# Turning twelve 128x512 tiles by blocks on VectorE and a trip through memory, or on TensorE

## The chip, the cores and the metric

The kernel runs on one core of one Trainium2 chip. The metric is the time of one execution in device microseconds. Three runs of the kernel before took 1243.22, 1246.52 and 1256.35 us; the median is 1246.52 us.

## The reference

Two layers work on eight sequences (B = 8) of 128 tokens of 512 values. The first is a per-sequence linear map, followed by a base linear layer with a gated mixture of eight low-rank experts. The second, in which the change lies, is attention over a paged cache followed by a gated low-rank layer:

```python
q, k = rope(rmsnorm(x @ Wq.T)), rope(rmsnorm(x @ Wk.T))   # 32 query heads, 8 key heads of 128
scores = q @ concat(k_cache[pages], k).T * SCALE           # 512 cached keys and 128 new ones
o = softmax(where(valid, scores, -1e30)) @ concat(v_cache[pages], v)
y = o.reshape(b, s, 4096) @ Wo.T                           # the attention's output, 128 x 512 per sequence
gate = softmax over the top 16 of (y @ Wq_w.T) @ keys.T    # 64 experts
z_gated = (y @ A_w.T).reshape(64, 8) * gate
x = x + (z_gated @ B_w.T) * SCALING
```

For each sequence the second layer's last part needs two tiles with their axes exchanged: y (the attention's output) ahead of the products with the router and A_w, and z_gated ahead of the product with B_w. TensorE contracts over the partitions, so a 128x512 tile with tokens on the partitions has to be turned into four 128x128 pieces with features on the partitions.

## The kernel before, in words

All engines follow an order written out by hand: each engine executes its instructions in the order in which the program records them.

The attention is cut into 64 units (NU). A unit is one sequence and one key head; there are four passes (NQ) over the eight sequences, with two key heads (GH) in each pass. A step `st` is one sequence of one pass, `st = u // 2`. The function `iteration(u)` (called for u = 0 to 66) overlaps the stages of several units:

- The scores of unit u on TensorE, for four query heads (`scores`, L793 and L796), each into one of two PSUM buffers of two banks. VectorE adds the mask and takes the minimum (`mask_exp`, L806), which frees the buffer; ScalarE takes the exponential (L817); GpSimd divides by the sum (`normalize`, L823).
- VectorE then turns the probabilities by blocks of 32x32 (`blocks`, L828), and `exchange_out` writes them to DRAM in four DMAs, two issued by SP and two by ScalarE (tile `px`, L840). In the next iteration `exchange_in` loads them back on SP with the blocks at their exchanged places (`pT`, L853). The turned queries and keys of unit u + 2 travel in the same way and are loaded first (`qkb`, L850); ScalarE copies them into order in `heads_qk` (L860) in iteration u + 1, ready for the scores of iteration u + 2.
- `values` (L873) multiplies the turned probabilities of unit u - 2 with the cached values, at the end of an iteration. ScalarE copies the result out of PSUM (`evict_o`, L884), and `output` (L895) multiplies it with Wo. After a step's second head `add_output` (L916) adds the new partial sum to that of the earlier passes; earlier passes keep theirs in DRAM (`yd`, `load_y`, L143). In the last pass the finished y of sequence b appears in iteration 52 + 2b.
- The projections for later units (`project`, L259 and L262), their norms (`norms`: squares on ScalarE L308, then `rs` on GpSimd L312 and L314) and the rotation on VectorE (`rotate`, L326 to L344; `rotate_k`, L340, needs `rs`) fill the rest.
- SP loads the cached key pages with one small DMA each (`gather`, L194), after it has read the page's number (L193).

The last layer begins while the attention still runs. `LAST` places sequence b = 0 to 6 in iteration 59 + b: `f_turn` turns y with four transposes on TensorE into PSUM (L684), which ScalarE copies to `yT` (L686); `f_project` makes the router's scores (L692) and z (L701); `f_gate` on VectorE, with one exponential on ScalarE (L724), makes `zg` (L733). In iterations 59 to 63 `f_turn` stands at the third head, later at the beginning. `z_turn` turns `zg` by four more transposes (L746) and a copy (L748), in iteration 65 and 66 for sequences 0 and 1 and in the tail for the others. The tail's `f_second` multiplies with B_w (L1130), adds the first layer's x (L1137) and writes the result (L1140).

The tile `y_home`, free from iteration 50 on, holds the finished y of sequences 0 to 3 and later the turned z of 0 and 1. The tile `xo` holds the projections' left operands; the last projection reads it in iteration 58. The tile `rooms` holds `zg` and the small tiles of the gate.

A DMA that SP or ScalarE issues signals one of eight completion semaphores. The program assigns them in turn over both queues, and a DMA waits for the one that used its semaphore before, unless that is known to be done.

Of the kernel before, what the change touches and what calls it, by code (L numbers as in the profile page):

```python
# [9 lines left out]
F32 = mybir.dt.float32  # L10
I32 = mybir.dt.int32
AF = mybir.ActivationFunctionType
ALU = mybir.AluOpType
# [3 lines left out]
P = 128  # L17
B = 8
S = 128
DM = 512  # L20
NC = DM // P
# [9 lines left out]
GH = 2  # L31
NQ = HKV // GH
HW = NH // 2 * D + D
QD = P // 32
# [23 lines left out]
def adaln_ffn_kernel(  # L58
# [25 lines left out]
    nc = tc.nc  # L84
# [49 lines left out]
    xo = keep.tile([P, B // 2, 7, 2, S], F32, name="xo")  # L134
# [4 lines left out]
    ya_t = {}  # L139
# [43 lines left out]
    def gather(step, first=0, end=NPP):  # L183
        hf, b = divmod(step, B)
        if first == 0:
            kv_t[step] = (
                kvp.tile([P, NPP, GH, PSIZE], F32, tag="kt", name=f"kt_{step}"),
                kvp.tile([P, LC, GH * D], F32, tag="vt", name=f"vt_{step}", bufs=3),
            )
        kt, vt = kv_t[step]  # L190
        for j in range(first, end):
            at = b * NPP + j
            page = nc.sync.value_load(pg[0:1, at : at + 1])  # L193
            nc.sync.dma_start(  # L194
                out=kt[:, j, :, :].rearrange("p g t -> p (g t)"),
                in_=kc[hf, ds(page, 1)].rearrange("o p f -> p (o f)"),
            )
# [17 lines left out]
    def bank(tag, name):  # L215
        return ps_1.tile([P, DM], F32, tag=tag, name=name)
# [454 lines left out]
    def f_fold(psum):  # L671
# [5 lines left out]
            )  # L677
        nc.vector.tensor_copy(fw_t["s"], rk)

    def f_turn(b, sb, psum):  # L680
        yb = ya_t.pop((NQ - 1) * B + b)
        tp = psum("tp", [P, NC, S])
        for c in range(NC):
            nc.tensor.transpose(tp[:, c, :], yb[:, c * P : (c + 1) * P], ident)  # L684
        yT = sb("yT", [P, NC, S])
        nc.scalar.copy(yT, tp)  # L686
        return yT
# [52 lines left out]

    zT_t = {}

    def z_turn(b, tp, sb):
        zg = zg_t.pop(b)
        for c in range(NC):
            nc.tensor.transpose(tp[:, c * S : (c + 1) * S], zg[:, c * P : (c + 1) * P], ident)  # L746
        zT = sb("zT", [P, NC, S])
        nc.scalar.copy(zT.rearrange("p c s -> p (c s)"), tp)  # L748
        zT_t[b] = zT


    with ExitStack() as l1:
# [150 lines left out]
        def add_output(u):  # L903
            st, g = units[u]
            del oT_t[u]
            if g % GH < GH - 1:
                return
            y = y_t.pop(st)
            last = st >= (NQ - 1) * B
            if g < GH:  # L910
                ya_t[st] = yp.tile([P, DM], F32, tag="ya", name=f"ya_{st}")
                nc.vector.tensor_copy(ya_t[st], y)
            else:

                t = y_home[st % B] if last and st % B < 4 else ya_t[st]
                nc.vector.tensor_tensor(t, y, ya_t[st], ALU.add)  # L916
                ya_t[st] = t
            if not last:
                nc.sync.dma_start(out=y_d[st % B], in_=ya_t.pop(st))

# [1 line left out]

        LAST = {NU - 5 + b: b for b in range(B - 1)}
        y_home, yT_t, room_t = {}, {}, {}

        def rooms():
            w = wp.tile([P, 7 * 2 * HW], F32, tag="wqkv", name="rooms", bufs=GH)
# [31 lines left out]
        def iteration(u):  # L959

            on = lambda v: 0 <= v < NU
            fb = LAST.get(u)
            r, group = u % 16, (u // 16 + 1) * GH
            f = room(fb) if fb is not None else None

            if u % 4 == 3:
                k, j, four = (u + 5) // 4, 0, True
            elif u % 4 == 0:
                k, j, four = (u + 4) // 4, 0, False
            elif u % 4 == 1:  # L970
                k, j, four = (u + 3) // 4, 1, True
            else:
                k, j, four = (u + 2) // 4, 1, False
            slots = ()
            if 2 < u and k < NU // 4:
                slots = (1, 2, 6) if four else (4, 5, 3)
            st = u // GH
            pages = on(u) and 1 < st + 1 < NQ * B
            first, end = ((0, 10), (10, NPP))[u % GH]
            if pages:  # L980
                gather(st + 1, first, first + 3)
            if on(u - 1):
                exchange_in(u - 1)
            if pages:
                gather(st + 1, first + 3, end)
            if pages:
                gather_v(st + 1, u % GH * LC // GH, (u % GH + 1) * LC // GH)
            if on(u + 3) and u % GH == 1:
                make_tables(units[u + 3][0])
            if u % GH == 0 and B <= st - 1 < NQ * B:  # L990
                load_y(st - 1)
            if on(u - 3):
                evict_o(u - 3)
            if u >= NU and fb is not None:
                yT_t[fb] = f_turn(fb, *f)
            if u > NU:
                z = u - NU - 1
                z_turn(z, bank("q" if z else "kv", f"ztp_{z}"), lambda n, shape: y_home[
                    z
                ].rearrange("p (c s) -> p c s", c=NC))  # L1000
            for h in range(REP):
                if on(u):
                    scores(u, h)
                    mask_exp(u, h)
                    if h > 0:
                        normalize(u, h - 1)

                    if h == 1:
                        if u == 2:
                            rotate(4)  # L1010
                        elif u == 3:
                            sums_q(1, 3, 2)
                        elif u == 4:
                            sums_q(1, 4, 1)
                        elif r in (10, 11, 12, 13) and u < NU - 8:
                            sums_q(group + r // 12, *((3, 2), (4, 1))[r % 2])
                    if h == 2:
                        new_pb(u)
                        if u + 2 in range(3, NU):
                            blocks_qk(u + 2, u)  # L1020
                    if h > 1:
                        blocks(u, h - 2)
                    if h == 1 and u == NU - 5:
                        f_fold(f[1])
                    if h == 2 and fb is not None:
                        yT_t[fb] = f_turn(fb, *f)
                if on(u - 3):
                    output(u - 3, h)
                if h > 0 and slots:
                    project(k, j, slots[h - 1 : h])  # L1030

                if u < 3 and h in (1, 3):
                    project_whole(1, *[(0, 1, h // 2), (1, h // 2, 1), (1, h // 2, 0)][u])
            if on(u - 3):
                add_output(u - 3)
            if on(u + 1) and (u + 1) % GH == 0:
                make_mask(units[u + 1][0])
            if u + 1 in range(3, NU):
                heads_qk(u + 1)

            if u < NU - 8:
                if r in (8, 9, 10, 11):
                    load_q(group + r // 10, r % 2, r % 2 + 2)
                if r in (12, 13):
                    load_o(group, r % 2 * 2, r % 2 * 2 + 2)
            if 16 < u < NU and r in (1, 2):
                load_o(group - 1, r * 2 - 2, r * 2)
            if NU - 8 < u < NU - 2:
                f_weights(u - NU + 7)
            if u == 2:  # L1050
                sums_q(0, 1)
            if on(u):
                normalize(u, REP - 1)
            if u == 0:
                norms(4)
            elif 4 < u + 3 < NU:
                norms(u + 3)
            if on(u):
                blocks(u, REP - 2)
                blocks(u, REP - 1)  # L1060
                exchange_out(u)
            if 4 < u + 3 < NU:
                rotate(u + 3)
                if four and slots:
                    project(k, j, (7,))

            if u in (2, 5, 7, 9):
                sums_x({2: 2, 5: 3, 7: 0, 9: 1}[u])
            if u == NU - 14:
                t = wp.tile([P, 4 * DM], F32, tag="wo", name="y_home", bufs=GH + 1)  # L1070
                y_home.update({b: t[:, b * DM : (b + 1) * DM] for b in range(4)})
            if u == NU - 6:
                rooms()
            if fb is not None:
                f_gate(fb, *f_project(fb, yT_t.pop(fb), *f), *f)
            if on(u - 2):
                values(u - 2)

# [6 lines left out]
    with ExitStack() as l2:  # L1085
# [31 lines left out]
        def f_turn_z(t):  # L1117
            b = t
            sb = lambda n, shape: p2.tile(shape, F32, tag=n, name=f"f{n}_{b}")
            z_turn(b, bank("q" if t % 2 else "kv", f"ztp_{t}"), sb)  # L1120

        def f_second(t):
            b = t
# [114 lines left out]
```

## Time and profile before

| | before |
|---|---|
| median of three runs | 1246.52 us |
| the profiled execution | 1243.45 us |
| its span, first to last instruction | 1241.7 us |
| TensorE busy | 1224.1 us, 99% |
| VectorE busy | 902.4 us, 73% |
| ScalarE busy | 506.6 us, 41% |
| GpSimd busy | 590.7 us, 48% |
| granted TensorE clock | 0.997 |
| DMA | 298.99 MB, 241 GB/s on average |
| exchange out `px`, issue to landing | 5.5 us (SP), 6.4 us (ScalarE) |
| exchange in `pT`, `qkb` | 6.6 us, 3.4 us |

The profile gives the busy time of each engine as a share of the span. Matmuls are pipelined: a row's own duration is longer than the time by which it moves the next one, so what a matmul costs is read from the chain of waits. That chain is followed back from the last instruction, at each step to what released it; time off this chain costs nothing until it grows enough to get on it. The profile's iterations near the end begin at 1087.7 us (59), 1105.8 (60), 1122.6 (61), 1139.4 (62), 1156.2 (63), 1173.1 (64), 1186.1 (65) and 1199.2 (66 has its y matmuls from here, and the tail follows).

### The profile page before, as it was taken

The numbers are of one execution on the slowest core, as the hardware profiler recorded it, in microseconds if no ns is written. First come the engines' busy times: TensorE is split into PE (matmuls) and PEld (weight loads), VectorE is DVE, ScalarE is ACT, GpSimd is POOL, SyncE is SP. The second block draws the span as 40 slices with busy tenths as digits, with TensorE's granted clock in tenths as the row PEclk, the third lists the DMA queues.
The fourth block names the chain that finished last, engine by engine and source line by source line (L and its number), as shares of the span: only waits on it lengthen the run. The fifth ranks groups of instructions, "written<-read, shape, count | busy, mean of one in ns | idle before, by whom it ended". The sixth has DMA issues, their size and how long they took to land.

```text
span 1241.7 us, 15991 instructions
## 1 busy us (share of the span) xinstructions
PE 1224.1 (99%) x3847; PEld 650.6 (52%) x3847; DVE 902.4 (73%) x2045; ACT 506.6 (41%) x1457; POOL 590.7 (48%) x687
## 2 busy tenths in 40 slices
PE   8999899999999999999999999999999999999998
PEld 7765455554555555555455555554555555555444
DVE  2546798889877777788877777788777777787522
ACT  1334444444444444444444444444444444443211
POOL 2443565575544555555445545655445544553100
PEclk9999999999999999999999999999999999999999
DMA  8822777788878877888878778888878777787512
GB/s 303 304 79 94 223 233 249 234 274 286 271 234 257 259 244 249 284 277 281 266 258 268 252 243 260 287 284 275 257 242 281 248 235 231 259 269 269 178 51 85
DMA packets 204785, 298.99 MB, mean 241 GB/s; under 512 B 84563, under 2 KB 116564, under 8 KB 203796
## 3 DMA queue, kind: packets, MB, share of 16 engines
q1 hardware_dynamic: 173092, 205.41, 52.6%
q10 hardware_dynamic: 18720, 52.49, 12.0%
q0 software_dynamic: 12880, 40.08, 9.4%
q8 instruction: 31, 0.51, 0.2%
q14 instruction: 62, 0.51, 0.1%
HBM read 183.54 MB, written 114.36 MB: 240 GB/s over the span
## 4 chain that ended last, share of the span: by engine, by line
PE 88%; DVE 4%; DMA 3%; ACT 2%; issue 1%; POOL 1%; ACTq 1%; SPq 0%; DVEq 0%; POOLq 0%
PE o L873 19%; PE p L259 18%; PE y L895 16%; PE s L793 16%; PE s L796 4%; PE p L292 2%; PE bp L517 2%; PE op L1130 2%; PE cp L495 2%; PE fz L701 2%; DMA px<-pb 1%; DVE wqkv L163 1%; ACT sq L308 1%; DMA kt<-in_kc 1%; DVE p L806 1%
## 5 line engine op out<-in xcount | busy, mean ns | idle before, releaser
L823 POOL TENSOR_SCALAR p<-p,den 128x640 f32<-128x640 f32 x256 | 211.8, 827 | 424.0 <-DVE den L822 423.4
L817 ACT ACTIVATE p<-p,low 128x640 f32<-128x640 f32 x256 | 212.0, 828 | 437.3 <-DVE den L822 297.4
L806 DVE CUSTOM_DVE_ANT_0 p<-s,mask,rs 128x640 f32<-128x640 f32 x256 | 224.0, 879 | 109.1 <-PE s L796 106.0
L259 PE MATMUL p<-wqkv,xo 128*128 128x384 f32 x784 | 280.4, 486 | 0.0
L895 PE MATMUL y<-wo,oT 128*128 128x512 f32 x512 | 262.5, 597 | 5.4 <-ACT oT L884 5.4
L793 PE MATMUL s<-kt,qkT 128*128 128x512 f32 x504 | 258.6, 595 | 3.2 <-ACT qkT L860 2.7
L873 PE MATMUL o<-pT,vt 128*128 128x512 f32 x512 | 230.2, 592 | 0.0
L259 PEld LDWEIGHTS p<-wqkv,xo 128*128 128x128 f32 x784 | 148.9, 190 | 139.8 <-issue 73.1
L828 DVE STREAM_TRANSPOSE pb<-p 128x640 f32<-128x640 f32 x252 | 207.7, 824 | 16.9 <-POOL p L823 16.9
L796 PEld LDWEIGHTS s<-qkT 128*128 128x128 f32 x504 | 96.2, 191 | 121.1 <-issue 121.1
L873 PEld LDWEIGHTS o<-pT,vt 128*128 128x128 f32 x512 | 97.3, 190 | 110.3 <-issue 95.2
L204 POOL DMA_INDIRECT vt<-in_vc,vrow x128 | 135.9, 1062 | 39.3 <-issue 27.7
L793 PEld LDWEIGHTS s<-kt,qkT 128*128 128x128 f32 x504 | 95.5, 191 | 98.2 <-issue 55.0
L314 POOL TENSOR_TENSOR rs<-ss,mhalf 128x5 f32<-128x5 f32 x64 | 99.7, 1558 | 5.3
L308 ACT ACTIVATE sq<-c 128x128 f32<-128x128 f32 x320 | 98.8, 309 | 8.1
L796 PE MATMUL s<-qkT 128*128 128x128 f32 x504 | 97.2, 275 | 0.0
L884 ACT COPY oT<-o 128x512 f32<-128x512 f32 x64 | 37.5, 586 | 144.8 <-PE o L873 139.4
L895 PEld LDWEIGHTS y<-wo,oT 128*128 128x128 f32 x512 | 78.6, 192 | 11.4 <-ACT oT L884 6.8
L262 DVE TENSOR_TENSOR c<-c,p 128x384 f32<-128x384 f32 x84 | 45.3, 539 | 31.2 <-PE p L259 31.2
L873 PE MATMUL o<-pT,vn 128*128 128x512 f32 x128 | 65.4, 592 | 0.0
L308 ACT ACTIVATION_READ_ACCUMULATOR sq<-c 128x1 f32 x320 | 59.7, 186 | 0.0
L779 DVE STREAM_TRANSPOSE pb<-ca 128x640 f32<-128x640 f32 x61 | 50.5, 828 | 6.8 <-DMA px<-pb 5.9
(181 smaller groups left out, 1178.9 us busy)
## 6 DMA issues: line engine op xcount, KB each, us to landing
pT<-px SPq DMA_DIRECT2D x64, 1280.0 KB, 6.6
px<-pb SPq DMA_DIRECT2D x122, 400.0 KB, 5.5
px<-pb ACTq DMA_DIRECT2D x122, 400.0 KB, 6.4
qkb<-px SPq DMA_DIRECT2D x61, 320.0 KB, 3.4
kt<-in_kc SPq DMA_DIRECT2D x512, 32.0 KB, 4.6
wqkv<-in_wqkv POOLq DMA_DIRECT2D x32, 384.0 KB, 5.1
yd<-ya SPq DMA_DIRECT2D x24, 256.0 KB, 3.1
wo<-in_wo POOLq DMA_DIRECT2D x12, 512.0 KB, 4.5
```

Source lines behind the costliest of these rows:

```text
L204: nc.gpsimd.indirect_dma_start(out=kv_t[step][1][:, c, :], out_offset=None, in_=vc, in_offset=bass.IndirectOffsetOnAxis(ap=vrow[:, hf, at ...
L259: nc.tensor.matmul(out=ps, lhsT=xo[:, pr, x, c, :], rhs=w[:, c, :], start=(c == 0), stop=(c == 1))
L308: nc.scalar.activation(sq, cs[:, at : at + D], AF.Square, accum_out=ss[:, h : h + 1])
L314: nc.gpsimd.tensor_tensor(rs, ss, mhalf, ALU.pow)
L793: nc.tensor.matmul(out=s[:, :L], lhsT=qkT[:, h, :], rhs=kt[:, :, g % GH, :], start=True, stop=True)
L796: nc.tensor.matmul(out=s[:, L:NK], lhsT=qkT[:, h, :], rhs=qkT[:, REP, :], start=True, stop=True)
L806: nc.vector.tensor_tensor_reduce(out=p, in0=s_t.pop((u, h))[:, :NK], in1=mask_t[st], scale=rs_t[u][:, h : h + 1], scalar=BIG, op0=ALU.add, ...
L817: nc.scalar.activation(p, p, AF.Exp, bias=low, scale=-1.0, accum_out=den)
L823: nc.gpsimd.tensor_scalar(p_t[u, h], p_t[u, h], den, 1.0, ALU.mult, ALU.mult)
L828: nc.vector.transpose(pb_t[u][:, :, h * w : (h + 1) * w].rearrange("p i (j a) -> p j i a", a=32), p_t.pop((u, h)).rearrange("p (j i a) -> ...
L873: nc.tensor.matmul(out=o, lhsT=vt[:, c, j * D : (j + 1) * D] if c < LC else vn_t.pop(u), rhs=pT[:, c], start=(c == 0), stop=(c == LC),)
L895: nc.tensor.matmul(out=y_t[st], lhsT=oT_t[u][:, h, :], rhs=wo_t[g][:, h, :], start=(h == 0 and j == 0), stop=(h == REP - 1 and j == GH - 1),)
```

## The change

For sequences 0 to 5 (`TURNED`) both y and zg are turned in another way. VectorE exchanges each 32x32 block's axes in one instruction (`turn_blocks`), four DMAs on SP write the result to DRAM with rows of 512 bytes, one DMA on SP loads it back with the blocks at their exchanged places (`turn_in`), and ScalarE copies it into the order of the matmuls (`turn_chunks`). Sequences 6 and 7 still go through TensorE.

The turn of y follows directly on the unit's `exchange_out` in iteration 52 + 2b, that of zg on the gate in iteration 59 + b. The load back stands in the next iteration after SP's page loads. The turned blocks of y 0 to 3 lie in `y_home`, those of y 4 and 5 and of all zg in `xo`; the sum L916 now stays in its own tile.

```diff
+    def turn_blocks(n, rows, room, pool):
+        nc.vector.transpose(
+            room.rearrange("p (k c a) -> p c k a", k=QD, c=NC),
+            rows.rearrange("p (c k a) -> p c k a", c=NC, k=QD),
+        )
+        m = pool.tile([QD, 32, QD, NC * 32], F32, tag="yx", name=f"yx_{n}")
+        for i in range(QD):
+            nc.sync.dma_start(
+                out=m[:, :, i].rearrange("k b f -> b k f"),
+                in_=room[i * 32 : (i + 1) * 32].rearrange("p (k f) -> p k f", k=QD),
+            )
+        blocks_t[n] = m, room
+
+    def turn_in(n):
+        m, room = blocks_t.pop(n)
+        nc.sync.dma_start(
+            out=room.rearrange("p (i f) -> p i f", i=QD), in_=m.rearrange("k b i f -> (k b) i f")
+        )
+        turned_t[n] = room
+
+    def turn_chunks(n, out):
+        nc.scalar.copy(
+            out.rearrange("p c (i a) -> p c i a", a=32),
+            turned_t.pop(n).rearrange("p (i c a) -> p c i a", i=QD, c=NC),
+        )
...
     def f_turn(b, sb, psum):
+        if ("y", b) in turned_t:
+            yT = sb("yT", [P, NC, S])
+            turn_chunks(("y", b), yT)
+            return yT
...
-    def z_turn(b, tp, sb):
+    def z_turn(b, sb):
         zg = zg_t.pop(b)
+        if ("z", b) in turned_t:
+            zT = zT_t[b] = sb("zT", [P, NC, S])
+            turn_chunks(("z", b), zT)
+            return
+        tp = bank("q" if b % 2 else "kv", f"ztp_{b}")
...
-                t = y_home[st % B] if last and st % B < 4 else ya_t[st]
-                nc.vector.tensor_tensor(t, y, ya_t[st], ALU.add)
-                ya_t[st] = t
+                nc.vector.tensor_tensor(ya_t[st], y, ya_t[st], ALU.add)
...
             if pages:
                 gather(st + 1, first + 3, end)
+            for n in list(blocks_t):
+                turn_in(n)
...
                 exchange_out(u)
+            b = (u - 3) // GH - (NQ - 1) * B
+            if on(u - 3) and (u - 3) % GH and 0 <= b < TURNED:
+                place = y_home[b] if b < 4 else spare[:, (b + 2) * DM : (b + 3) * DM]
+                turn_blocks(("y", b), ya_t.pop((NQ - 1) * B + b), place, dram_x)
...
                 f_gate(fb, *f_project(fb, yT_t.pop(fb), *f), *f)
+                if fb < TURNED:
+                    turn_blocks(("z", fb), zg_t[fb], spare[:, fb * DM : (fb + 1) * DM], dram_x)
```

More of the change, by code (lines that the diff above doesn't have):

```diff
@@ L678, in f_fold @@
         nc.vector.tensor_copy(fw_t["s"], rk)
+    blocks_t, turned_t = {}, {}
+    TURNED = B - 2
+    def turn_blocks(n, rows, room, pool):
[21 more added lines that the diff above has]
+        )
     def f_turn(b, sb, psum):
+        if ("y", b) in turned_t:
+            yT = sb("yT", [P, NC, S])
+            turn_chunks(("y", b), yT)
+            return yT
         yb = ya_t.pop((NQ - 1) * B + b)
@@ L924, in adaln_ffn_kernel @@
         y_home, yT_t, room_t = {}, {}, {}
+        spare = xo.rearrange("p r x c s -> p (r x c s)")
         def rooms():
@@ L997, in iteration @@
                 z = u - NU - 1
-                z_turn(z, bank("q" if z else "kv", f"ztp_{z}"), lambda n, shape: y_home[
-                    z
-                ].rearrange("p (c s) -> p c s", c=NC))
+                z_turn(z, lambda n, shape: y_home[z].rearrange("p (c s) -> p c s", c=NC))
             for h in range(REP):
@@ L1119, in f_turn_z @@
             sb = lambda n, shape: p2.tile(shape, F32, tag=n, name=f"f{n}_{b}")
-            z_turn(b, bank("q" if t % 2 else "kv", f"ztp_{t}"), sb)
+            z_turn(b, sb)
         def f_second(t):
```

## The prediction

> **What bounds the kernel now.** I read the busy shares first, then the chain of waits over the last 150 us, then the timelines of VectorE, ScalarE and the SP queue where the change works. The page:
>
> ```profile
> PE 1224.1 (99%) x3847; PEld 650.6 (52%) x3847; DVE 902.4 (73%) x2045; ACT 506.6 (41%) x1457; POOL 590.7 (48%) x687
> ...
> PE 88%; DVE 4%; DMA 3%; ACT 2%; issue 1%; POOL 1%; ACTq 1%; SPq 0%; DVEq 0%; POOLq 0%
> ```
>
> TensorE is the bound and is almost never idle. The granted clock is 0.997 throughout, so only removed matmul time or new stalls count. The chain (start, length, what) shows the pieces to be removed:
>
> ```profile
> 1093.92 0.44 PE ftp L684 x4
> ...
> 1173.13 0.59 ACT oT L884
> 1173.72 0.04 issue
> 1173.76 3.70 PE y L895 x8
> ...
> 1186.08 0.44 PE ftp L684 x4
> 1186.52 0.44 PE ztp L746 x4
> 1186.95 3.56 PE y L895 x8
> ...
> 1199.22 0.59 ACT oT L884
> ```
>
> A sequence's four transposes cost 0.44 us of chain. Two groups are not in it: turning y 5 (near 1173) and z 1 (near 1199) stands beside the ScalarE copy L884, for which the next y matmul waits anyway. Iteration u of the loop starts at its first scores: 59 at 1087.7, 60 at 1105.8, 61 at 1122.6, 62 at 1139.4, 63 at 1156.2, 64 at 1173.1.
>
> Three timelines (start, length) around iterations 59 and 60 show the slack: VectorE,
>
> ```profile
> 1107.65 0.69 DVE L733 TENSOR_TENSOR rooms<-fz,rooms 128x512 f32<-128x512 f32 x1
> 1108.26 0.88 DVE L806 CUSTOM_DVE_ANT_0 p<-s,mask,rs 128x640 f32<-128x640 f32 x1
> ```
>
> ScalarE,
>
> ```profile
> 1098.34 0.71 ACT L860 COPY qkT<-qkb 128x640 f32<-128x640 f32 x1
> ```
>
> and SP's queue:
>
> ```profile
> 1094.44 0.53 SPq L850 DMA_DIRECT2D qkb<-px  x1
> ...
> 1108.50 0.54 SPq L850 DMA_DIRECT2D qkb<-px  x1
> ```
>
> VectorE goes from the gate straight into the first mask step (L806) of iteration 60, which ends at 1109.14; its PSUM bank is what the third head's scores need, and they start at 1109.49. That is 0.35 us of slack. In iteration 61 it is 1126.05 against 1126.31. The qkb load needs 3.4 us to land, so the one of 1094.44 lands 0.5 us before ScalarE copies it.
>
> **What is removed.** By the order of the instructions 48 TensorE transposes go (12 groups), 12 VectorE transposes and 60 DMAs on SP (48 out, 12 back) come. The gains by the chain:
> - y 0 to 4, in iterations 59 to 63: 5 x 0.44 = 2.2 us.
> - y 5 and z 1: nothing, as above.
> - z 0 at 1186.52: the y matmuls would start at 1186.78 (end of the L884 copy, 1186.17 + 0.59 + 0.02) instead of 1186.95: 0.2 us.
> - z 2 to 5, between output matmuls with no gap: 4 x 0.44 = 1.76 us. ScalarE's copies from memory come earlier than those from PSUM, none is late.
> Together 4.1 us, with 5.2 us (12 x 0.44) as the upper bound. The 128x128 transpose has rows of 272 ns each, but four take 0.44 us, so 0.11 us of the chain each. The Trainium skill ("TensorE: Matmul & The Clock Gate", Part 4: PE-mode transpose) gives about 275 ns in a kernel's context; that is the row, but 48 x 0.275 = 13.2 us would be three times what the chain gives back. The Trainium skill ("VectorE: DVE Perf Modes", Rules for kernel authors) would leave a 128x128 transpose on TensorE where PSUM may receive it, against this change; no row of before weighs the two, as only what TensorE waits for decides here.
>
> **What is added on VectorE and ScalarE.** A 128x640 block transpose steps by 0.74 us (L828), so 128x512 takes 0.59. The six of y follow the last blocks of an even iteration; there rotate_k waits 0.5 us (iterations 52 to 58) or 1.4 us (60) for POOL's rs, and the later mask step has over 2 us to its bank, so nothing reaches TensorE. The z ones stand between the gate and the mask step: 0.35 us of slack in 60 and 0.26 in 61 are overrun, in 62 and 63 VectorE idles 2.6 and 3.0 us before that step. ScalarE's copies of 128x512 keep their number; the permuted one takes 0.57 (L860: 0.71 for 640) where the PSUM one takes 0.57.
>
> **What is added on SP's queue.** Every hardware DMA signals one of eight semaphores in turn, and waits for the DMA that used it before. In the order of the changed program this does three things:
> 1. After each y turn (even iterations), four out-DMAs stand ahead of the next iteration's three page loads and its qkb load, and those page loads now wait for the exchange px, eight places back. An issue costs 0.4 us (rows 0.33 to 0.42). Before, the page loads were issued while px was on its way; now they come after it, 0.68 us each. Iteration 53: qkb 994.29 becomes about 996, lands 999.4, and was copied at 999.45: hidden. In 55 and 57 alike (slack 1.7). In 59 the px landing (7.4 us from 1086.51) lets the first load go at 1093.9, three make it 1095.6 instead of 1094.44: 1.15 us late, 0.65 over the slack. The copy, the norms, rs, rotate_k, the gate and the mask step of 60 all follow it.
> 2. The four z out-DMAs of iteration 59 wait on SP for the VectorE turn, which is after the gate: 1108.3 + 0.65 + 0.66 = 1109.6, issued by 1111.2. Behind them are three page loads (2.0 us as after an exchange; 5.1 us, the stretch 987.7 to 992.8, while one is in flight; I take 2.8, nearer to the first since px has landed) and qkb, so 1114.0 instead of 1108.50, landing 1117.4 where it was copied at 1115.16: 2.3 us late, with 1.4 to 4.5 as ends.
> 3. The load back of z 0 in 60 waits for ScalarE's first px DMA of 60, and SP's own two px DMAs are queued behind it. Px goes out in two steps, its halves one landing (4.6 us) apart, then the z 1 out-DMAs, page loads and qkb for 62: about 1137 to 1140, where it was 1125.41 + 3.4. The copy ran at 1131.98, but its reader, the scores of 62, came at 1139.4. This uses nearly all of that cover; I cost it at nothing.
>
> **The sum.** Iteration 60, third head: the bank is free at 1109.14 + 0.59 + 0.65 + 0.25 (from mask end to scores, the waiting weight load included) = 1110.6; TensorE would be there at 1109.49 - 0.44 = 1109.05; stall 1.6. Iteration 61: free at 1126.05 + 0.25 + 0.59 + 2.3 = 1129.2; TensorE would be there at 1126.31 - 0.88 + 1.6 = 1127.0; stall 2.2 (1.3 to 4.4). Lost 3.8, gained 4.1: net -0.3 us. The profiled execution took 1243.45 us (its span 1241.7), so 1243 us. It is 3 us under the median of the three runs, 1246.52, whose spread (1243.22 to 1256.35) is larger than the change; I stay with 1243 and let the range reach up.
>
> **The rivals.**
> - *A clean gain.* The page loads go out fast and POOL's rs, not qkb, still sets the gate; only the turns' 0.59 us overrun. By the sum's formula without the 0.65 and the 2.3 they make stalls of 0.9 and 0.5 us; with the ready bank used a little sooner, none. 1243.45 - 4.1 + 0 to 1.5 = 1239.3 to 1240.9. For it: landings vary from 4.1 to 7.4 us, and SP waits for px 98 us in 76 waits, so it has time. Against it: only 1.2 to 1.4 us of wait remain at the qkb loads of 53 to 59.
> - *The exchange falls behind: slower.* One mechanism: the px of 60 in two steps. If a landing takes 7.4 us (the row of 1086.5) and three page loads 5.1, then ScalarE's px of 60 lands at 1127.5, SP's at 1136.5, qkb goes at 1142 and is copied by 1146.3; the scores of 62 are due at 1139.4 + 2.5 = 1141.9, so 4.4 us are lost. The point is a landing of qkb after 1141.2; from there each us is a us of TensorE. SP's second px of 61 then waits for ScalarE's px of 61, which stands behind that copy: the scores of 63 lose some 3 us more. With the stalls of 60 and 61 at their upper end (6.5): -4.1 + 6.5 + 7.4 = +9.8, 1253 us; +12.4 is needed for 1%, so two landings must be longer yet.
> - *The change does nothing*: excluded by the order of the instructions, which lacks the 48 transposes.
>
> **How the numbers follow.** A measurement of this kernel tells 1% (12 us) from no change. Forecast (1241 to 1246): 0.5. Clean gain (1238 to 1241, 5.2 us being the bound): 0.25. Exchange behind: 0.25, with 0.08 of it beyond 1%. Faster by over 1% would need more than twice the transposes' whole time: 0.01. Within 1%: 0.91. Range 1238 to 1252: it takes in the clean gain, the forecast with both ends of the page loads, the runs' own spread, and most of the third case.
>
> **What would show it.** PE loses 48 instructions and 5.2 us of chain. Idle time of TensorE before the third scores of 60 and 61 with the mask step as releaser, about 1.6 and 2.2 us: right. Gate-to-mask order with a 0.6 us transpose between. The qkb issue of 60 near 1114 and of 61 near 1135 on the old clock. The chain runs through VectorE and SP there. Wrong, if TensorE is idle in 62 or 63 at the first scores (the third case), if the tail from 1199 does not shrink by 1.76, or if the copies of y 5 (due 1177) wait for its load back.

## The result, and the profile after

The changed kernel took 1253.99 us (median of six runs, 1253.02 to 1257.56); the kernel before, on the same chip, 1244.05 us (1242.75 to 1256.35). The ratio is 1.0076, with a 95% interval of 1.0053 to 1.0099: slower by 0.8%, within the 1% that the prediction called no change, but 11 us over the predicted 1243 and 2 us over the range. The profiled execution took 1257.56 us, its span is 1255.6 us. It is the longest of the six, and 1.2 us of its difference arise ahead of iteration 52, where the two programs are the same.

The page of the changed kernel, busy times and shares of the chain of waits:

```profile
PE 1224.8 (98%) x3799; PEld 646.5 (51%) x3799; DVE 908.8 (72%) x2057; ACT 507.2 (40%) x1457; POOL 590.2 (47%) x687
...
PE 84%; DMA 4%; DVE 4%; SPq 2%; ACT 2%; issue 2%; POOL 1%; ACTq 0%; DVEq 0%; POOLq 0%
```

TensorE has its 48 instructions fewer, is busy as long as before (a stretch at a slower clock, below, is in that), and is idle for 30.8 us of the span instead of 17.6. The list of what TensorE waited for, from 1000 us on (us in total, times, longest us); before, the same list from 900 us on held one line, 0.6 us of `y` for `oT`:

```profile
PE s L834 <- DMA xo<-yx_('y', 4)_9493: 7.5, 1, 7.5
PE y L936 <- ACT oT L925: 4.5, 5, 1.9
PE s L834 <- DVE low L847: 1.0, 2, 0.5
PE s L834 <- DMA px<-pb: 0.8, 1, 0.8
PE s L834 <- DMA kt<-in_kc: 0.4, 1, 0.4
```

To see where each belongs I cut the span at the first `o` row (L873 before, L914 after) of each iteration. These matmuls stand at an iteration's end, so "iteration u" below is the stretch from the first `o` row of iteration u - 1 to that of u, with the scores of u at its start. After minus before, in us: iteration 54 +1.01, 59 -0.44, 60 +3.19, 61 +1.45, **62 +9.39**, 63 -0.44, the stretch from the last of these rows (1194.68 before) to the end -1.52; all others are within 0.03. The sum is +12.7, in the longest of the six executions; the medians differ by 9.9. Iteration 62 carries three quarters of it. TensorE's timeline there (start, length; in brackets the idle time before the row and what ended it):

```profile
1144.86 1.02 PE L914 MATMUL o<-pT,vn 128*128 128x512 f32 x2
1153.41 2.05 PE L834 MATMUL s<-kt,qkT 128*128 128x512 f32 x2 [7.52 <-DMA xo<-yx_('y', 4)_9493]
1155.25 0.64 PE L837 MATMUL s<-qkT 128*128 128x128 f32 x2
1155.67 1.92 PE L936 MATMUL y<-wo,oT 128*128 128x512 f32 x2
1157.38 1.12 PE L834 MATMUL s<-kt,qkT 128*128 128x512 f32 x2
```

The releaser in brackets is inferred from what landed at that moment. The scores read neither `xo` nor `yx`. They read `qkT`, which ScalarE had copied by 1146.16, and the key tile `kt`, whose last three pages SP issued just ahead of that load back. The last of them landed 8.4 us after its issue, at 1153.0; the load back landed at 1153.4, as the scores started:

```profile
L194 SPq DMA_DIRECT2D kt<-in_kc x1: 430/430/430, 1144.6 to 1144.6; - x1
...
DMA to landing us min/median/max: 8.4/8.4/8.4
```

SP's queue in the kernel before (start, length, the DMAs of a row):

```profile
1125.41 0.53 SPq L850 DMA_DIRECT2D qkb<-px  x1
...
1127.13 2.02 SPq L194 DMA_DIRECT2D kt<-in_kc  x3
```

and after:

```profile
1114.05 1.77 SPq L692 DMA_DIRECT2D yx_('z', 0)_9366<-xo  x4
1116.41 2.07 SPq L194 DMA_DIRECT2D kt<-in_kc  x3
1118.58 0.53 SPq L891 DMA_DIRECT2D qkb<-px  x1
...
1130.43 0.86 SPq L881 DMA_DIRECT2D px<-pb  x2
1131.39 5.15 SPq L692 DMA_DIRECT2D yx_('y', 4)_9493<-xo  x4
1136.63 1.86 SPq L692 DMA_DIRECT2D yx_('z', 1)_9530<-xo  x4
1139.02 2.07 SPq L194 DMA_DIRECT2D kt<-in_kc  x3
1141.19 0.54 SPq L891 DMA_DIRECT2D qkb<-px  x1
1141.82 0.57 SPq L894 DMA_DIRECT2D pT<-px  x1
1142.91 2.11 SPq L194 DMA_DIRECT2D kt<-in_kc  x3
1145.07 0.72 SPq L700 DMA_DIRECT2D xo<-yx_('y', 4)_9493  x1
```

Three things are to be seen. The three pages behind `pT`, here at 1142.91, were issued at 1127.13 in the kernel before, 12.3 us ahead of the scores of 62; here it is 3.0 us ahead of the moment at which TensorE was ready for them. The four out-DMAs of y 4, right behind `px`, take 5.15 us; the four of z 1, issued when those were out, take 1.86. And the `qkb` load is at 1118.58 in iteration 60 and 1141.19 in 61, where it was at 1108.50 and 1125.41.

The windows around the wait (stretch, its length, busy us and instructions of PE, PEld, DVE, ACT, POOL, then the granted TensorE clock as a share of full speed, DMA share, GB/s):

```profile
1127.00:1145.70 18.70, 17.34 (x52) 8.18 (x50) 14.30 (x45) 5.16 (x12) 5.71 (x7) 1.00 0.78 217
1145.70:1153.40 7.70, 0.18 (x1) 0.02 (x1) 2.27 (x6) 1.29 (x3) 0.00 (x0) 0.83 1.03 365
1153.40:1158.40 5.00, 4.99 (x9) 2.46 (x10) 0.89 (x2) 0.92 (x2) 0.00 (x0) 0.58 0.73 172
1158.40:1163.30 4.90, 4.90 (x17) 2.45 (x16) 3.33 (x8) 2.35 (x5) 1.60 (x2) 1.00 0.99 351
```

The idle time costs a second time: for 5 us after it TensorE ran at a granted clock of 0.58. On the chain the first scores took 2.03 us where the next pair took 0.91, and the first `y` pair 1.71 where the next took 0.86, some 2.2 us in all. So 7.5 + 2.2 - 0.44 = 9.3 us of the 9.39. The Trainium skill ("TensorE: Matmul & The Clock Gate", Why this matters for your kernels) asks for no idle gap above some 3 us between matmul bursts, or the clock falls to 4/8; the windows agree with 0.58 after a gap of 7.5 us. The length of the gap alone does not decide it here: in e3_pages_early below the clock was 1.00 in the 5 us after a gap of 3.67 us (at 1119.62), in e9_z_out_late 0.66 in the 5 us after one of 2.01 us (at 1111.83).

VectorE and ScalarE at the gate of iteration 60, the rows that answer to those of before:

```profile
1112.58 0.69 DVE L769 TENSOR_TENSOR rooms<-fz,rooms 128x512 f32<-128x512 f32 x1
1113.31 0.71 DVE L686 STREAM_TRANSPOSE xo<-rooms 128x512 f32<-128x512 f32 x1
1113.94 0.84 DVE L847 CUSTOM_DVE_ANT_0 p<-s,mask,rs 128x640 f32<-128x640 f32 x1
```

```profile
1103.78 0.72 ACT L901 COPY qkT<-qkb 128x640 f32<-128x640 f32 x1 [2.40 <-DMA qkb<-px]
...
1110.40 0.35 ACT L760 ACTIVATE rooms<-rooms 128x64 f32<-128x64 f32 x1 [3.57 <-DVE rooms L752]
1110.66 0.56 ACT L925 COPY oT<-o 128x512 f32<-128x512 f32 x1
```

With the turn between them the mask step starts 1.36 us after the gate's last instruction, where it was 0.61: it moves by 0.75 us. On ScalarE the copy of `qkb` waits 2.40 us, and the copy of `o` that TensorE's next `y` matmul needs (L925) stands behind the gate's exponential (L760). That order is the 1.9 us of `y` in iteration 60.

The chain in the last layer (start, length, what):

```profile
1205.94 0.84 PE fr L728 x8
1206.78 3.49 PE fz L737 x8
1210.27 4.31 PE o L914 x10
```

No transposes are left there; the stretch to the end is 1.52 us shorter.

### The profile page after: what moved, and what is told of

It reads as the page before. It is cut to its first block, busy times and chain, and to the rows that moved or that the text cites. A ratio compares the mean times of both kernels' runs of the same rounds, so it can differ in the third digit from the quotient of the medians.

```text
span 1255.6 us, 15985 instructions
## 1 busy us (share of the span) xinstructions
PE 1224.8 (98%) x3799; PEld 646.5 (51%) x3799; DVE 908.8 (72%) x2057; ACT 507.2 (40%) x1457; POOL 590.2 (47%) x687
## 4 chain that ended last, share of the span: by engine, by line
PE 84%; DMA 4%; DVE 4%; SPq 2%; ACT 2%; issue 2%; POOL 1%; ACTq 0%; DVEq 0%; POOLq 0%
PE p L259 18%; PE o L914 18%; PE y L936 16%; PE s L834 16%; PE s L837 4%; PE p L292 2%; PE op L1175 2%; PE bp L517 2%; PE cp L495 2%; DMA px<-pb 2%; PE fz L737 1%; SPq L692 1%; DMA kt<-in_kc 1%; DVE pb L869 1%; ACT sq L308 1%
## 5 line engine op out<-in xcount | busy, mean ns | idle before, releaser
L914 PE MATMUL o<-pT,vt 128*128 128x512 f32 x512 | 230.2, 592 | 0.0
L914 PEld LDWEIGHTS o<-pT,vt 128*128 128x128 f32 x512 | 97.3, 190 | 110.3 <-issue 95.2
L314 POOL TENSOR_TENSOR rs<-ss,mhalf 128x5 f32<-128x5 f32 x64 | 95.3, 1489 | 5.3
L925 ACT COPY oT<-o 128x512 f32<-128x512 f32 x64 | 37.4, 584 | 135.7 <-PE o L914 129.6
L914 PE MATMUL o<-pT,vn 128*128 128x512 f32 x128 | 65.4, 592 | 0.0
```

The source lines that it names most:

```text
L314: nc.gpsimd.tensor_tensor(rs, ss, mhalf, ALU.pow)
L914: nc.tensor.matmul(out=o, lhsT=vt[:, c, j * D : (j + 1) * D] if c < LC else vn_t.pop(u), rhs=pT[:, c], start=(c == 0), stop=(c == LC),)
```

## The experiments

All ratios are to the kernel before, run on the same chip beside the experiment, with their 95% interval. "Sum" is what the profiled execution gained or lost from the first `o` row of iteration 52 on, against the one profile of the kernel before, by the lengths of the iterations as above. Ahead of that row two profiles of the same code differ by up to 10 us, and timed runs of one kernel by up to 14, so the sum is sharper than a ratio; but it is of one execution each, and in e6, e9 and e11 it lies 2 to 3.5 us above what the timed medians differ by.

| run | what is turned on VectorE, and how | ratio | sum, us | iteration 60, 61, 62 | end |
|---|---|---|---|---|---|
| changed kernel | y 0-5, z 0-5 | 1.0076 [1.0053, 1.0099] | +12.7 | +3.19, +1.45, +9.39 | -1.52 |
| e1_y_only | y 0-5 | 1.0015 [0.9992, 1.0037] | +2.0 | +2.02, -0.38, -0.44 | +0.14 |
| e2_z_only | z 0-5 | 1.0065 [1.0041, 1.009] | +8.1 | +0.54, +1.24, +7.89 | -1.58 |
| e3_pages_early | all, pages moved | 1.012 [1.0079, 1.0162] | +14.7 | +4.29, +1.39, +2.49 | -1.49 |
| e4_turn_only | all, without DMAs | 0.9988 [0.9963, 1.0014] | -1.1 | +1.47, +0.34, -0.25 | -1.79 |
| e5_z_back_late | all, z back from 63 | 1.0075 [1.005, 1.0099] | +11.1 | +2.20, +1.43, +8.52 | -1.54 |
| e9_z_out_late | all, z out from 62 | 0.9996 [0.9975, 1.0016] | +3.0 | +3.50, +0.34, -0.43 | -1.52 |
| e10_pool_queue | all, DMAs on GpSimd | 1.0277 [1.0247, 1.0307] | +34.2 | +7.52, +9.62, +4.39 | -1.76 |
| e6_own_slots | all, DMAs moved | 0.9983 [0.9966, 0.9999] | +1.1 | +1.86, +1.07, -0.43 | -1.48 |
| e7_z_own_slots | z 0-5, moved | 1.0 [0.998, 1.0019] | -1.6 | 0, 0, 0 | -1.59 |
| e8_tail_z | z 2-5, moved | 0.9986 [0.9971, 1.0002] | -1.5 | 0, 0, 0 | -1.55 |
| e11_y01 | y 0-1, z 2-5, moved | 0.998 [0.9965, 0.9995] | +0.1 | +1.83, +0.34, 0 | -1.63 |
| e12_y01_again | the same | 0.9982 [0.9967, 0.9997] | -1.0 | -0.04, +0.33, 0 | -1.56 |

The theories of the first four: A, SP's queue is late, and with it the key pages that the next step's scores read; B, the exchange of q and k is late by itself; C, VectorE's added turns lie on the chain.

**Each half alone.** e1_y_only leaves z to TensorE, e2_z_only leaves y to it:

```diff
# e1_y_only
-                if fb < TURNED:
-                    turn_blocks(("z", fb), zg_t[fb], ...)
# e2_z_only
-            if on(u - 3) and (u - 3) % GH and 0 <= b < TURNED:
+            if False:
```

> Only y of the six sequences is turned by blocks; z_gated goes through TensorE as before. Theory A (SP's queue is late with the cached key pages, above all the last three of step 31 ahead of the scores of unit 62): the out-DMAs of y still take 5.5 us of SP behind an exchange, so about 1.0 us stays lost at unit 54 and 2 to 3 us in iteration 60, but the pages of step 31 are late by one group of out-DMAs only, 0 to 2 us of stall at unit 62; with 2.2 us of transposes gone 1245 to 1248 us. Theory B (the late exchange of queries and keys by itself holds up unit 62): the same delay of qkb by 5 us, 1250 us. Theory C (VectorE's added turns lie on the chain): half of the turns, about half of the loss, 1249 us.

> Only z_gated of the six sequences is turned by blocks; y goes through TensorE and stays in its old tile. Theory A: SP waits for the gate and the turn ahead of the pages, and the load back of z 0 waits for ScalarE's half of the exchange, so the pages of step 31 are 5 to 8 us late: 2 to 5 us of stall at unit 62, 1 to 3 us in iterations 60 and 61, 2.0 us of transposes gone: 1246 to 1250 us. Theory B: 1249 us. Theory C: 1249 us. It tells A from the others by which wait stands ahead of the scores of unit 62, not by the sum.

The y half costs 2.0 us, the z half 8.1, and together they cost 2.6 more than the two added. What was expected of the z half was far too little: its loss is again in iteration 62. So y's out-DMAs are not needed for it, though they make it larger.

**The last pages moved.** e3_pages_early issues thirteen pages of the next step in an even iteration and three in the odd one, from iteration 52 on:

```diff
-            first, end = ((0, 10), (10, NPP))[u % GH]
+            first, end = ((0, 13), (13, NPP))[u % GH] if u >= 52 else ((0, 10), (10, NPP))[u % GH]
```

> The changed kernel, but from iteration 52 on thirteen pages of a step are loaded in the even iteration and three at the start of the odd one, none behind its qkb and pT. Theory A: the waits ahead of the scores of units 54, 60 and 62 lose the pages (1.0, 0.4 and 7.5 us, and the 2 us of matmuls at a lower granted clock that follow the longest), at unit 62 only the copy of the turned queries is left, 0 to 2 us: 1243 to 1246 us. Theory B: the scores of unit 62 still wait for the exchange, 1251 to 1254 us. Theory C: no change, 1254 us.

The forecast of the time was wrong, the wait was told right. TensorE's waits in this run, from 1000 us on:

```profile
PE y L936 <- ACT oT L925: 12.6, 10, 3.7
PE s L834 <- ACT qkT L901: 2.7, 1, 2.7
...
```

The wait for a DMA at the scores of 62 is gone; the next one there, 2.7 us, is for the copy of `qkb`. With the landing at 1153.0 above, that is the evidence that it had been the pages: of what those scores read, nothing else was moved forward. But ten pages in a row now stand ahead of `px` on SP in the even iterations (8.62 us from 1089.41 on, the `px` DMAs at 1099.72 instead of right after `pT`'s seven pages), every later `qkb` is late, and ten `y` matmuls wait for ScalarE. Iterations 55 to 61 are each 0.9 to 4.3 us longer. At this place SP's queue had no room for three more pages.

**The turns without the DMAs.** e4_turn_only leaves out the 60 DMAs, so that the blocks stay at their wrong places:

```diff
-        for i in range(QD):
-            nc.sync.dma_start(out=m[:, :, i]..., in_=room[i * 32 : (i + 1) * 32]...)
...
-        nc.sync.dma_start(out=room..., in_=m...)
```

> The changed kernel with VectorE's twelve turns and ScalarE's copies, but without the 60 DMAs: the blocks are not exchanged through memory, so the gated products of six sequences use blocks at wrong places. Theories A and B: without SP's added work no page and no exchange is late; left are 4.1 us of transposes gone and 0.9 + 0.5 us of stalls from the two turns ahead of a mask step: 1241 to 1242 us. Theory C: 1250 us or more.

C falls: with all turns and copies in place the loss is gone. But of the 4.1 us that the prediction booked as gain only 1.1 come back, where 0.9 and 0.5 us of stalls were expected. The waits of this run:

```profile
PE y L927 <- ACT oT L916: 1.8, 3, 0.7
PE s L825 <- DVE low L838: 1.0, 2, 0.5
PE y L927 <- ACT rooms L751: 0.9, 1, 0.9
```

The first row stands in iterations 64 to 66, beside the transposes of y 5, z 0 and z 1, which the prediction had booked at nothing or nearly so. The other two stand in iterations 60 and 61, where, by these rows, the gate's chain (VectorE with z's turn in it, the exponential and the mask step) sets the time and not TensorE's own work. Four transposes less for TensorE don't shorten that chain: here y 1 and y 2 give nothing, y 0, 3 and 4 give 0.44, 0.25 and 0.44. In e1_y_only, without z's turn, iteration 61 is 0.38 shorter, so there y 2 does pay. A part of the 1.47 us of iteration 60 is a late landing of `px`, of which more below.

**What makes SP late.** My theory after the first four runs was the load back of z 0. On SP it waits in iteration 60 for ScalarE's half of `px`, with SP's own half behind it. e5_z_back_late takes it out of iterations 60 to 62:

```diff
-                turn_in(n)
+                if n[0] == "y" or u > 62:
+                    turn_in(n)
```

> The changed kernel, but the turned z is loaded back from iteration 63 on only (before: from iteration 60 on); nothing is left out. Theory A says that the load back of z 0, which waits on SP in iteration 60 for ScalarE's half of the exchange px and has SP's own px queued behind it, is what makes the qkb load and the last key pages of step 31 late: without it the wait of TensorE at the first scores of iteration 62 falls from 7.5 us to 0 to 3 us, its clock there stays above 0.95, and the time is 4 to 9 us under that of the changed kernel: 1245 to 1250. Rival D says that it is the out-DMAs of z, four in each odd iteration, that wait for the gate and keep SP from the exchange: then the wait at iteration 62 stays at 6 us or more, and the time within 2 us of the changed kernel's 1254.

That theory fell. TensorE's wait in 62 is still there,

```profile
PE s L834 <- DMA xo<-yx_('y', 4)_9492: 5.8, 1, 5.8
...
```

and iteration 62 is 8.52 us longer. SP's waits from 1100 to 1160 us in the changed kernel show the other candidate (theory D below), the z out-DMAs that stand on SP until the gate and the turn are done:

```profile
SPq L881 <- DMA pT<-px: 7.2, 2, 4.3
SPq L692 <- DVE xo L686: 6.5, 1, 6.5
SPq L194 <- DMA kt<-in_kc: 2.7, 1, 2.7
...
```

e9_z_out_late leaves all else as changed and issues the out-DMAs of z 0 to 2 in iteration 62, behind the last pages:

```diff
+            if u >= 62:
+                for n in list(waiting_t):
+                    turn_out(n)
...
-                    turn_blocks(("z", fb), zg_t[fb], ..., dram_x)
+                    turn_blocks(("z", fb), zg_t[fb], ..., dram_x, u >= 62)
```

> The changed kernel with its y part, its turns and its loads back as they are; only the out-DMAs of z 0 to 2, which stand on SP behind the gate in iterations 59 to 61, are issued in iteration 62, behind the last key pages (their loads back follow in 63). Nothing is left out. Theory D (SP standing still for the gate of iteration 59 starts the lateness that reaches iteration 62): the wait at the first scores of iteration 62 goes from 7.5 us to below 1.5, the granted clock there stays above 0.95, iteration 62 is at most 1.5 us longer than before; the waits that the y part brings in iterations 54 and 60 (some 3 us) remain and the tail keeps its gain of 1.5: ratio 0.999 to 1.003, 1244 to 1250. If it is the sum of all DMAs on SP, whatever they wait for, iteration 62 stays at least 4 us longer than before and the ratio is 1.004 or more.

D holds: iteration 62 is 0.43 us shorter than before, as the removed transposes would have it, and the clock in the 5 us after 1146 is 1.00. Nothing else than the place of twelve out-DMAs was changed, and with it that of three loads back, which e5 had moved alone. It is not their number either, as SP still issues them all. What no run parts is the wait of z 0's out-DMAs for the gate (6.5 us) from the time that those of z 0 and z 1 take to issue (1.8 us each): e9 moved both away. What remains at the scores are waits of the y half, the first and third row here (the second stands in 64 to 66 as in e4):

```profile
PE s L840 <- DMA kt<-in_kc: 2.0, 1, 2.0
PE y L942 <- ACT oT L931: 1.8, 3, 0.7
PE s L840 <- DMA y_home<-yx_('y', 2)_8920: 1.0, 1, 1.0
...
```

The wait of 2.0 us is in iteration 60; the slower clock after it (0.66 over 5 us, an estimated 1.7 us of matmul time) makes the rest of its 3.5 us.

So out-DMAs that held SP in iteration 59, 6.5 us of it in waiting, reached TensorE three iterations later. Each iteration has one exchange through SP (`px`, `qkb`, `pT` and six or ten pages), and from 60 to 61 the queue did not catch up: against the first `o` row of the iteration before, `qkb` was 8.2 us later than before the change in iteration 60 and 10.8 us in 61.

**Another queue.** e10_pool_queue lets GpSimd issue all 60 DMAs (`nc.sync` to `nc.gpsimd` in `turn_blocks` and `turn_in`).

> The changed kernel with all 60 DMAs of the turns issued by GpSimd and none by SP, each at its place in the order. Nothing is left out. Theory A: SP's qkb and page loads are back at the places of the kernel before, so the waits at the first scores of 54, 60 and 62 (0.8, 0.4 and 7.5 us) are gone. GpSimd pays for it: its row for a plain DMA is 0.8 us, so 3 to 5 us for four, behind which the divisions of p (two of 0.8 us an iteration) and rs stand, and the z ones wait for the gate there as well; this can cost 0 to 2 us in each of the iterations 59 to 63. Ratio 0.998 to 1.004. If the loss is not in SP's queue but in the memory traffic itself (60 DMAs with rows of 512 bytes beside the exchange), the wait at 62 stays at 4 us or more and the ratio at 1.005 or more.

The half about SP holds: no scores wait for a page any more. The half about GpSimd missed by far, 1.0277. The rows of GpSimd's waits from 1000 to 1200 us:

```profile
...
POOL y_home L700 <- DMA yx_('y', 3)_9205<-y_home: 6.2, 1, 6.2
...
POOL yx_('z', 0)_9366 L692 <- DVE xo L686: 6.1, 1, 6.1
...
POOL y_home L700 <- DMA yx_('y', 2)_8920<-y_home: 5.9, 1, 5.9
...
```

The four issues are cheap there (2.3 us), but each load back in this list waits 5 to 6 us on GpSimd until its out-DMAs have landed, and the value gathers, the divisions of `p` and `rs` are queued behind it. I had counted the issues and not that wait. The Trainium skill ("DMA: Bandwidth & Descriptors", Issuing engines are not separate DMA queues) says that issuing from several engines saves only the time to initiate a DMA, which it calls usually small beside the DMA itself. Here it wasn't: behind `px` one issue of 64 KB held SP for 1.3 to 1.4 us, where such a DMA took 3.3 to 6.9 us to land, and the four of a y held it for 5.2 to 5.6 us.

**Places where SP and VectorE have time.** In e6_own_slots the y out-DMAs go into the next odd iteration, behind `qkb`, `pT` and the pages; z is turned an iteration later at the place behind `exchange_out`, and its DMAs begin in 62:

```diff
+            if u % GH or u >= 62:
+                for n in list(blocks_t):
+                    turn_in(n)
+                for n in list(waiting_t):
+                    if n[0] == "y" or u >= 62:
+                        turn_out(n)
...
+            if u - 60 in TURNED_Z:
+                z = u - 60
+                turn_blocks(("z", z), zg_t[z], ..., dram_x, u >= 63)
```

e7_z_own_slots keeps of it z 0 to 5, e8_tail_z z 2 to 5, e11_y01 and e12_y01_again z 2 to 5 with y 0 and 1.

> All six sequences turned on VectorE as in the changed kernel, but every DMA of it stands where SP waits for nothing: the out-DMAs of y in the next, odd iteration behind the qkb load and the last three pages, their load back one odd iteration later; z is turned one iteration later at the place behind exchange_out, so not between the gate and the mask step, and its DMAs begin in iteration 62, after the last pages. Nothing is left out. Theory A (SP's queue) expects most of the removed transposes' time to come back: no wait above 0.6 us at the first scores of iterations 54, 60 and 62, the iterations 59 to 63 each 0 to 0.44 us shorter than before, the tail 1.5 shorter, in all 2 to 3.5 us under the kernel before, ratio 0.997 to 0.9985. If the 4.1 us cannot be had even so (rival E: the copies of the turned blocks and the turns themselves stand in the way of VectorE and ScalarE), the ratio is 0.999 to 1.002.

> As the run with own slots, but only z of six sequences is turned on VectorE; y goes through TensorE as before. Nothing is left out. Theory A: the tail is 1.5 to 1.8 us shorter, iterations 52 to 61 as before within 0.3 us each, no wait in 62: 1.5 to 2 us under the kernel before, ratio 0.998 to 0.999. Rival E: the turns moved beside exchange_out still cost VectorE enough for the mask steps of 61 to 63 to be late, 0.5 to 1.5 us, and the ratio is 0.999 to 1.001.

> As the run with own slots, but only z of sequences 2 to 5 is turned on VectorE, those whose four transposes stand between the output matmuls of the tail; y, z 0 and z 1 go through TensorE as before. Nothing is left out. Theory A: all of the gain of the tail, 1.5 to 1.8 us, and nothing else moves: ratio 0.998 to 0.999. Rival E: below 0.8 us of gain, ratio 0.9993 or above.

> As the run with own slots, but only y 0 and 1 and z 2 to 5 are turned on VectorE: those whose DMAs fall in iterations in which SP had time. Nothing is left out. Theory A: iterations 59 and 60 each 0.44 us shorter, the tail 1.55 shorter, no wait of TensorE above 0.5 us in 53 to 62: 2 to 2.4 us under the kernel before, ratio 0.998 to 0.9985. If the y DMAs cost TensorE something even there, iteration 55 or 60 is 0.5 to 2 us longer and the ratio 0.999 to 1.000.

> The kernel with y 0 and 1 and z 2 to 5 in their own slots once more, for a second profile and a second comparison; nothing is left out. In the first profile iteration 60 was 1.83 us longer than before because the exchange px of iteration 58 landed 0.9 us later than in the runs without a turned y. If that is chance (landings of this exchange from 7.6 to 9.3 us after its issue are found in the runs so far), this profile has an even chance to show iterations 59 and 60 both 0.44 us shorter, and the ratio is again 0.998 with 1 outside or at the edge of the interval. If it belongs to the turned y, iteration 60 is again at least 1 us longer, the sum from iteration 52 on is within 0.5 us of zero, and the ratio 0.999 to 1.001.

z in its own place gives most of the 1.76 us that the prediction booked for the tail, 1.55 to 1.6 us, and nothing else moves; z 0 and z 1 add nothing. The timed ratios of e7 and e8 (1.0 and 0.9986, 1 within both intervals) can't see 1.6 us. With y 0 and 1 as well the ratio is 0.998 and 0.9982 in two comparisons, each with an interval that ends below 1: some 2 us faster than the kernel before, the only version here, with e6 (0.9983), of which that can be said. From e8 (0.9986) the ratios do not tell it, so a gain by y 0 and 1 is not shown. Its two profiles show that the y part is not a clean gain: iteration 59 is 0.44 us shorter in both, iteration 60 was 1.83 longer in one and 0.04 shorter in the other, and iteration 55 was 0.70 longer in the second alone. `qkb` of iteration 59 went out 12.7 us after the first `o` row of iteration 58 in the first profile, 11.7 in the second, 11.2 in the kernel before; from the issue of `px` on SP it was 8.9, 8.5 and 7.9 us. Why that landing varies stays open, and with it whether the loss in 60 is chance or belongs to the turned y.

## Why the prediction was wrong, step by step

- **The gains.** 0.44 us for iterations 59 and 63: measured, to 0.01. y 5 and z 1 nothing: right. z 0, booked 0.2: nothing, its iteration is unchanged within 0.03. The tail 1.76: 1.48 to 1.79 in the runs that turn z. Iterations 60 and 61 (y 1, y 2): booked 0.88, e4 shows none of it; by its waits the gate's chain, with z's turn in it, and not TensorE was late there. Without that turn y 2 gave 0.38 (e1) and y 1 0.04 (e12). So the step "y 0 to 4: 5 x 0.44" failed for y 1, and for y 2 beside z's turn. I had written down the slack of 0.35 and 0.26 us in just these iterations, which says that TensorE is only that much behind VectorE.
- **The turns on VectorE.** 0.59 us, hidden for y, overrunning the slack for z in 60 and 61: the order was right, the size 0.75 us at the mask step of 60. The stalls at the scores were 0.5 us each instead of 1.6 and 2.2, since the `y` matmul ahead of them waited first, 1.91 us in 60 and 0.84 in 61. The prediction followed `qkb` to the mask step and left out ScalarE's copy of `o`, which stands behind the exponential of the same gate.
- **SP, point 1: "An issue costs 0.4 us".** The term that was mis-sized. Behind `px` the four y out-DMAs took 5.2 to 5.6 us, 1.3 to 1.4 each; those of z 0, issued 6.6 us after the last `px`, 1.77, or 0.44 each. The page loads had shown such a cost in the profile of before: three while an exchange was in flight took 4.0 us, 5.1 with the pause ahead of them, and I had used that only as an upper end for pages. So `qkb` of 59 went out at 1099.58, not 1095.6 (three loads of 0.68 us from 1093.9 on make 1095.9); against the first `o` row of iteration 58 that is 2.9 us later than before, where 1.15 were booked. The delay in iteration 53, called hidden, cost iteration 54 1.0 us: `qkb` was in time there, the pages behind it were not.
- **SP, point 2: z 0 waits for the gate.** Foreseen, with `qkb` of iteration 60 at 1114.0; it was 1118.58 (1117.4 without the 1.2 us that arose ahead of iteration 52), because the gate itself was late with the `qkb` of point 1: the out-DMAs started at 1114.05 instead of 1109.6. The mechanism was right; where it ended was not.
- **SP, point 3: "I cost it at nothing".** The step that failed. `qkb` of 61 was put at 1137 to 1140; it went out at 1141.19, or 1140.0 without the 1.2 us from ahead of iteration 52: the late end of the forecast. Of the cause named, the load back of z 0 behind ScalarE's `px`, e5 leaves at most 1.7 us of TensorE's wait; the rest is point 2 carried on (e9). And `qkb` was the wrong thing to watch: its copy ended at 1146.16, 0.3 us after TensorE was ready. Behind it and `pT` SP issues the last three pages of step 31, which the same scores read, and these cost 7.5 us, with 2.2 more for the slow clock behind the gap. The prediction counted the page loads as time ahead of `qkb` and never as data that somebody waits for. Counted so, its own times would have told of the stall: in the profile of before the last of these pages is issued 3.4 us behind `qkb` (1128.8, 1125.4), and a page at that place in iteration 59 took 6.0 us to land (issued at 1097.0). With `qkb` at 1137 to 1140 that is, as an estimate, 1146.4 to 1149.4, where the third rival had the scores of 62 due at 1141.9.
- **The rivals.** "The exchange falls behind" had the place (the first scores of 62), the sign and nearly the time, 1253. It got there on another way: slow page loads and a late `qkb`, 4.4 us in 62 and 3 in 63, where slow out-DMAs and late pages made 9.4 in 62 and nothing in 63. It had no term for the clock, 2.2 us, and its 6.5 us for iterations 60 and 61 is more than the upper ends in the sum (1.6 + 4.4). That it came within 1 us of the median is in part luck. Against the forecast's 0.5 its 0.25 was too little: both rows that it was built on stood in the profile of before.
- **The chances.** Within 1% had 0.91, and 0.76% is within it, but not by the sum that stood behind it (-0.3 us); the range stopped 1 us short of that rival's 1253 and 2 us short of the median.

## What to carry to other kernels

Before a DMA is added to a queue, list every later instruction on that queue with the one who reads its data, and not only the transfer that the new one is about; a transfer that waits for a late engine makes all of them late, and a queue without slack keeps that: here it showed three iterations on. Price an issue by the rows at the same place, beside the same traffic. Taking work off TensorE gains only in iterations that TensorE itself bounds: where a gate or a mask step is within half a us, the next engine keeps the time.

## What the runs showed of the hardware

- Issuing four DMAs of 64 KB on SP took 1.77 to 1.86 us for z 0 and z 1 in the changed kernel and 5.15 to 5.58 us for y 0 to 4, right behind two `px` DMAs of 400 KB each (with ScalarE's half on its way as well). Behind `px` z 2 took 4.20 us; in e9, in a row behind `pT`, z 0 to 2 took 2.7 to 4.6, and y 4 at its old place 4.6 (e5) to 6.6 (e9).
- A page of 32 KB, issued behind the 1280 KB of `pT`, took 8.4 us to land in the stretch in which TensorE waited and the DMA share was 1.03.
- After 7.5 us without a matmul TensorE's granted clock was 0.58 over 5 us, and 1.00 in the 4.9 us after that; a pair of score matmuls that later took 0.91 us took 2.03. After gaps of 3.67 us (e3) and 2.01 us (e9) the clock over 5 us was 1.00 and 0.66.
- The named releaser of a long wait was a DMA whose data the waiting instruction doesn't read. It landed 0.4 us behind the last page, which the instruction does read.
- The exchange `px` of iteration 58, the same DMAs in all runs, let `qkb` go 7.6 to 9.3 us after its issue in the runs with no out-DMAs between the two, and at that place the kernel before had 0.5 us of slack (prediction, by the landing of 3.4 us).
